# A decoder kernel: the first products of five half tiles cut into 32 columns instead of 64, and another place for one weight tile

## The chip, the cores and the metric

The kernel is one program on one core of a Trainium2 chip. The core has a matrix engine (TensorE, PE in the profile, with PEld for its loading of weights), VectorE (DVE), ScalarE (ACT), GpSimd (POOL) and SyncE (SP), which mainly issues DMAs. The metric is the device time of one execution in microseconds; of several runs the median is given.

## The reference

Two decoder layers work on x of shape (8, 256, 256) in float32. The first has self attention, attention over a context and a choice of experts; the second has causal attention, attention over the context with a learned null key and value, and the feed-forward part that the change touches. That part takes the 2,048 tokens after a layer norm:

```python
scores_aE = x_aD @ router_DE
vals_aK, idx_aK = jax.lax.top_k(scores_aE, K)          # K = 1, E = 8 experts
gates_Ea = jax.nn.sigmoid(masked_aE).T
routed_in_EaD = gates_Ea[:, :, None] * x_aD[None, :, :]
mid_EaF = silu(einsum('ead,edf->eaf', routed_in_EaD, w1_eDF)) * einsum('ead,edf->eaf', routed_in_EaD, w3_eDF)
routed_out_EaD = einsum('eaf,efd->ead', mid_EaF, w2_eFD)
shared_aD = silu(x_aD @ ws1_DF) * (x_aD @ ws3_DF) @ ws2_FD
out_aD = shared_aD + routed_out_EaD.sum(axis=0)
```

D is 256 and F is 704. Every token goes through one expert of eight and through the shared expert, and x is added to the result.

## The kernel before, in words

**The last stage.** Tokens are sorted by expert into tiles of 128 rows. A tile either belongs to one expert as a whole (tiles 0 to 11) or is a half tile, with 64 rows of one expert and 64 of another (tiles 12 to 16). `slots` (L1858) goes through them in the order 0, 1, 12, 2, 3, 13, 4, 5, 14, 6, 7, 15, 8, 9, 16, 10, 11. For every tile `into` (L1829) makes the hidden layer and `outof` (L1842) the output rows, and the next tile's `into` stands ahead of this tile's `outof`. PE and SP run exactly in the order in which the code is written there; the other engines' order is a planner's. Every second tile two tiles of rows are turned by `turned` (xrp in the profile).

Within `into`, `hidden` (L1061) goes through six chunks of 128 hidden units, the last one half wide. A chunk needs two outputs h of 128 x 128 (for w1 and w3; the last has both in one, so there are 11 in all). `first` (L1833) makes an output as a sum over two chunks c of the input's 256 features. In a half tile this is done for each of its two sets of weights, with 64 tokens each. Each such product goes through `product` (L274), which cuts the 128 output columns of the weights into two matmuls of 64 columns on two halves of the output's partitions. The profile calls these "h<-xrT,w" at L276; 128*64 128x64 is a half tile's form, with 64 tokens, and 128*64 128x128 a full tile's. ScalarE then applies silu (sl, L1071), and VectorE multiplies (midr, L1072). `outof` multiplies by the second weights in products of 64 columns, 256 wide (out, L1846).

The weights come from HBM, packed by expert: `first_weights` (L1802) loads w1 and w3 of a set (w13, 1,408 KB) and `second_weights` (L1812) w2 (768 KB), on SP's queue. A half tile takes two sets. There are four buffers of each kind; a load is issued when PE has finished with the buffer that it reuses.

**`product4`** (L280) does what `product` does with four matmuls of 32 columns on four quarters of the output's partitions. It serves the attention (qk, v, ao, fm, vps in the profile at L282), the choice of experts in the first layer (lg, cs, rps, back) and other places. den (L1446) also has 32 columns.

**The shared expert's weights.** When the last of eight batches begins its attention over the context, the projection weights are no longer needed, and L1582 closes the pools that held them. On the right side of the memory they lay, from the top down, as ctxs (4,096 bytes a partition), wp (wkv_x 32,768 and wq_x 8,192, wkv_x below), kvs (kT and vx, 8,192 each, vx above kT), and wsum. L1583 opens a new pool, mids, in their place, with its top where that of ctxs was. Its first tile lies lowest. `load_shared` (L1054) makes its tiles in this order: ws13 (w1 and w3 of the shared expert, 11,776 bytes), two mid (12,288 each) and ws2 (the second weights, 6,144). The routing tables follow (4,448). `ended` (L1033) has POOL clear the part of the last chunk that the weights do not fill. `w_in` (L1025) loads ws13 on SP, `w_out` (L1038) loads ws2 there, later (L1603), and POOL copies 64 columns within ws13 (L1030). Names in the profile drop numbers: ws13 and ws2 both appear as ws, mid0 and mid1 as mid.

The shared expert's first products are hx (L1079) in that stretch, with silu and the products by seven (L1120) behind them; its outputs by ws2 are added at L1674. After the last tile PE makes the last quarter of the shared expert (L1079 and L1663).

Of the kernel before, what the change touches and what calls it, by code (L numbers as in the profile page):

```python
# [29 lines left out]
F32 = mybir.dt.float32  # L30
# [9 lines left out]
P = 128  # L40
B, S, D = 8, 256, 256
# [9 lines left out]
NFC = len(FCH)  # L51
# [106 lines left out]
def plain(  # L158
# [105 lines left out]
    def layernorm_T(b, work, mm, bufs=2):  # L264

        xn = work.tile([P, 2, D], F32, tag="xn", name="xn", bufs=bufs)
        mv, rs = norm_stats([x[:, 2 * b + t, :] for t in range(2)], 1e-5, small, "ln")
        for t in range(2):
            last = normed(xn[:, t, :], x[:, 2 * b + t, :], mv, rs, t)
        return last, transposed(xn, work, mm, "xnT", bufs=bufs)  # L270
# [3 lines left out]
    def product(out, lhsT, rhs, start, stop):  # L274
        return [
            nc.tensor.matmul(out[h], lhsT[:, h], rhs, start=start, stop=stop, skip_group_check=True)  # L276
            for h in (slice(0, 64), slice(64, P))
        ]
# [570 lines left out]
    def context(b):  # L849
        t = ctxs.tile([P, CTX // P, S], F32, tag="ctxT", name="ctxT")  # L850
        nc.sync.dma_start(t, a["ctx_T"][b].rearrange("(c p) t -> p c t", p=P))
        return t

    def key_room():
        return kvs.tile([P, nc8, S], F32, tag="kT", name="kTx")

    def value_room():
        return kvs.tile([P, 2, XH, XD], F32, tag="vx", name="vx")
# [166 lines left out]
    def w_in(pool, src1, src3, name):  # L1025

        t = pool.tile([P, 2, 2 * FF + tail], F32, name=name, tag=name)
        nc.sync.dma_start(t[:, :, :FF], src1.rearrange("(c p) f -> p c f", p=P))
        nc.sync.dma_start(t[:, :, FF + tail :], src3.rearrange("(c p) f -> p c f", p=P))
        nc.gpsimd.tensor_copy(t[:, :, FF : FF + tail], t[:, :, 2 * FF :])  # L1030
        return t

    def ended(t):  # L1033

        nc.gpsimd.memset(t[tail:, full, :], 0.0)
        return t

    def w_out(t, src):  # L1038
        nc.sync.dma_start(t[:, :full, :], src[: full * P].rearrange("(c p) d -> p c d", p=P))
        nc.sync.dma_start(t[:tail, full, :], src[full * P :])  # L1040
        return t
# [5 lines left out]
    shared = {}  # L1047
# [5 lines left out]

    def load_shared(pool):  # L1054

        shared["ws13"] = w_in(pool, a["L1_ffn_ws1_DF"], a["L1_ffn_ws3_DF"], "ws13")

        shared["mid_s"] = [ended(pool.tile([P, NFC, 2 * S], F32, name=f"mid{i}")) for i in range(2)]
        shared["ws2"] = ended(pool.tile([P, NFC, D], F32, name="ws2"))

    def hidden(mid, first, n, pair, silu):  # L1061

# [126 lines left out]
    def routed_norm(b, work):  # L1189

        xn = work.tile([P, 2, D], F32, tag="y", name="xne", bufs=1)
        mv, rs = norm_stats([x[:, 2 * b + t, :] for t in range(2)], 1e-5, small, "ln")
        for kept, v in zip(norms[b], (mv, rs)):
            nc.gpsimd.tensor_copy(kept, v)
        for t in range(2):
            normed(xn[:, t, :], x[:, 2 * b + t, :], mv, rs, t)
        return xn

    def routed_rows(b, xn, work):
        transposed(xn, work, mm, "", shared["xnT"][:, :, bass.ts(b, S)])  # L1200
# [87 lines left out]
    def null_cross_attention(phase):  # L1288
# [15 lines left out]
        def query_room():  # L1304
            return work.tile([P, nc8, S], F32, tag="qT", name="qTx", bufs=1)
# [20 lines left out]
        def w_terms(blocks, m):  # L1326

            ((b11, b12), (b21, b22)), (t1, t2, t3, t4) = blocks
            return [t[:, :, m, :] for t in (b11, b21, b22, t4, t1, t2, t3)]

        def sums_of_rows(rows, n, name, apart):


            def block(i, j):
                return rows[:, n * j : n * (j + 1), bass.ts(i, P)]

            sw = wsum.tile([P, 4 if apart else 3, n, P], F32, tag=name, name=name)
            s1, s2, s4 = (sw[:, i] for i in range(3))
            s3 = sw[:, 3] if apart else block(1, 0)
            nc.vector.tensor_tensor(s1, block(1, 0), block(1, 1), ALU.add)  # L1340
            nc.vector.tensor_tensor(s2, s1, block(0, 0), ALU.subtract)
            nc.vector.tensor_tensor(s4, block(0, 1), s2, ALU.subtract)
            nc.vector.tensor_tensor(s3, block(0, 0), block(1, 0), ALU.subtract)
            return block(0, 0), block(0, 1), s4, block(1, 1), s1, s2, s3
# [168 lines left out]
        def in_range():  # L1513

            for k in range(3):
                v = dens[:, k].rearrange("p t h -> p (t h)")
                low = work.tile([P, S], F32, tag="low", name="lowk", bufs=1)
                nc.vector.tensor_scalar(low, v, 1.0e-25, None, ALU.is_ge)
                nc.vector.scalar_tensor_tensor(
                    low, v, 1.0e25, low, ALU.is_le, ALU.mult, accum_out=fit[:, B + k : B + k + 1]  # L1520
                )
# [46 lines left out]
        for b in range(B):  # L1568
            more = b + 1 < B
            if more:  # L1570
                ctxT = context(b + 1)
            oT, den, rest = weighted(kT, v, qT)
            if more:
                _, xnT = layernorm_T(b + 1, work, mm, 1)
                if b:
                    xe = routed_norm(b - 1, work)
                of_ctx = sums_of_rows(ctxT, CTX // P // 2, "sw", False)
            else:
                xe = routed_norm(b - 1, work)
                rest()  # L1580

                wproj.close()  # L1582
                late = ctx.enter_context(tc.tile_pool(name="mids", bufs=1, side="right"))  # L1583
                load_shared(late)
                sums = phase.enter_context(tc.tile_pool(name="sums", bufs=1, side="right"))
                order.enter_context(tc.manual_schedule(engines={mybir.EngineType.PE}))
            if more:
                order.enter_context(tc.manual_schedule(engines={mybir.EngineType.PE}))
            if b:
                routed_rows(b - 1, xe, work)  # L1590
            if more:
                of_x = sums_of_rows(xnT, 1, "swq", True)
                kT, v, qT = key_room(), value_room(), query_room()
                k7 = seven("k7", of_ctx, w_terms(kv_blocks, 0), kT, False)
                v7 = seven("v7", of_ctx, w_terms(kv_blocks, 1), v, True)
                q7 = seven("q7", of_x, w_terms(q_blocks, 0), qT, False)
                next(k7)
                rest()
            rs, old = reciprocals(b, den, en), en
            if b == 1:  # L1600
                in_range()
            if not more:
                w_out(shared["ws2"], a["L1_ffn_ws2_FD"])  # L1603
                routing_tables(late)
            if more:

                for made in (k7, k7, v7, k7, k7, k7, v7, v7, q7, v7, q7, v7, v7, q7):
                    next(made)
            else:
                first = hidden_shared(0, pair, lambda n: spare()[:, 0, :n])  # L1610
                for i in range(4):
                    next(first)
                    if i == 0:
                        routed_scores(b - 1)
                shared["of_w"] = sums_of_shared(*(sums.tile([P, full * P], F32, name=f"tws{i}") for i in range(4)))
            divide(oT, rs, (nc.gpsimd, nc.gpsimd if more else nc.vector))
            outward(b, oT, old)
            if more:
                next(q7), next(q7)
                if b:  # L1620
                    routed_scores(b - 1)
                next(q7)
                en = null_key(xnT)
            else:
                for _ in first:
                    pass
            order.close()
# [11 lines left out]
    with ExitStack() as phase:  # L1639
        null_cross_attention(phase)  # L1640
# [3 lines left out]
    def token_experts(phase):  # L1644
# [5 lines left out]
        ws2, mid_s = shared["ws2"], shared["mid_s"]  # L1650
# [178 lines left out]
        def into(sets, xrT):  # L1829
            mid_r.append(mid_r.pop(0))  # L1830
            mid, n = mid_r[-1], P // len(sets)

            def first(h, lo):  # L1833
                for i, (w13, _) in enumerate(sets):
                    for c in range(2):
                        product(h[:, bass.ts(i, n)], w13[:, c, lo : lo + P], xrT[:, c, bass.ts(i, n)], c == 0, c == 1)

            for _ in hidden(mid, first, P, pair, silu):
                pass
            return mid  # L1840
# [64 lines left out]
        with tc.issue_after(last.ins), tc.manual_schedule(engines={mybir.EngineType.DVE}):  # L1905
            for i in range(4):
# [3 lines left out]
                if i:  # L1910
                    lo = group[0]
# [946 lines left out]
```

## Time and profile before

| What | us |
|---|---|
| median of 3 runs | 1198.14 |
| lowest and highest of them | 1196.61, 1200.52 |
| profiled execution, its own time | 1198.71 |
| its span, first to last instruction | 1197.0 |
| PE busy in the span | 1135.5 (95%) |
| DVE, ACT, POOL busy | 566.2, 447.5, 417.6 |
| expert tiles on PE, first to last product | 1021.3 to 1158.4 |
| loads of ws13 issued | 915.5 |

Times in the trace are counted from the span's start. A row of the chain of waits gives the start, the length and what ran; "issue" is time for which the profile shows no cause. A row of the groups by form gives line, engine, operation, the tiles written and read, the shape, and how often; then busy time, mean ns of one, idle time before and what ended it. For a matmul 128*64 128x64 means 128 rows and 64 columns of weights and 64 moving columns per partition. Each float32 matmul of the code stands as two in the records. Busy times are unions, and matmuls on different columns overlap, so busy time is less than the sum of the parts. A row of the windows gives the stretch, its length, the busy time and count of each engine (PE, PEld, DVE, ACT, POOL), the granted clock of PE (1.00 is full), the share of the 16 DMA engines and GB/s. In the list of queues stand packets, MB and the share of 16 engines.

### The profile page before, as it was taken

How to read it: one execution, taken by the hardware profiler on the slowest of the kernel's cores; microseconds unless marked ns; L12 is line 12 of the kernel's file. 1: busy time of each engine (PE TensorE's matmuls, PEld its weight loads, DVE VectorE, ACT ScalarE, POOL GpSimd, SP SyncE). 2: the span in 40 equal slices, each digit the busy share in tenths (PEclk: the TensorE clock that was granted, in tenths of full speed). 3: DMA queues.
4: the chain of work that ended last, by engine and by line, in shares of the span. 5: the costliest groups of instructions: out<-in, count | busy, mean ns of one | idle time of the engine just before them, and what ended most of it. 6: DMA issues, size and time to landing. Idle time of an engine off the chain costs nothing.

```text
span 1197.0 us, 31939 instructions
## 1 busy us (share of the span) xinstructions
PE 1135.5 (95%) x13788; PEld 706.5 (59%) x13788; DVE 566.2 (47%) x1564; ACT 447.5 (37%) x696; POOL 417.6 (35%) x482
## 2 busy tenths in 40 slices
PE   6898899998899999999999999999998999999996
PEld 2334444454445454666676767666664576888864
DVE  5465878778685643824241424242324473222213
ACT  3666665665443541314141414141413230222220
POOL 3245365455655730314141414141415114100013
PEclk9999999999999999999999999999998999999999
DMA  7046232130200600020202010101103007799924
GB/s 226 1 133 204 91 119 92 54 122 2 84 2 17 233 3 19 2 54 2 54 2 54 6 50 10 46 19 37 24 15 105 5 30 305 277 414 394 392 73 129
DMA packets 51446, 116.78 MB, mean 98 GB/s; under 512 B 8272, under 2 KB 36416, under 8 KB 46944
## 3 DMA queue, kind: packets, MB, share of 16 engines
q1 hardware_dynamic: 45120, 98.90, 24.0%
q0 software_dynamic: 3456, 12.73, 2.9%
q10 hardware_dynamic: 2720, 3.02, 0.7%
q8 instruction: 110, 1.80, 0.6%
q14 instruction: 40, 0.33, 0.1%
HBM read 104.00 MB, written 27.93 MB: 110 GB/s over the span
## 4 chain that ended last, share of the span: by engine, by line
PE 76%; POOL 7%; issue 6%; DVE 6%; ACT 4%; DMA 1%; SPq 0%; POOLq 0%; ACTq 0%; DVEq 0%
PE h L276 7%; PE k L276 6%; PE v L276 6%; PE wo L276 5%; PE ox L1470 5%; PE stx L1431 5%; PE st L334 4%; PE out L1846 4%; PE o L371 3%; PE out L1663 3%; PE h L1079 3%; PE qk L282 3%; PE q L276 3%; ACT pT L345 2%; PE den L1446 2%
## 5 line engine op out<-in xcount | busy, mean ns | idle before, releaser
L345 ACT ACTIVATE pT<-st 128x1024 f32<-128x1024 f32 (+1 forms) x128 | 110.7, 919 | 64.3 <-PE st L334 64.3
L371 PE MATMUL o<-pT,padv 128*32 128x256 f32 (+1 forms) x1536 | 99.7, 370 | 4.3 <-POOL pT L350 4.2
L371 PEld LDWEIGHTS o<-pT,padv 128*32 128x32 f32 x1536 | 40.6, 109 | 86.2 <-issue 37.5
L1437 POOL TENSOR_TENSOR both<-pTx 128x512 f32<-128x512 f32 x64 | 81.2, 1296 | 29.0 <-ACT pTx L1435 23.8
L276 PE MATMUL h<-xrT,w 128*64 128x128 f32 (+1 forms) x1936 | 87.0, 250 | 0.4 <-issue 0.4
L276 PEld LDWEIGHTS h<-xrT,w 128*64 128x64 f32 x1936 | 84.4, 137 | 3.3 <-issue 1.1
L345 ACT ACTIVATE pT<-st,kbias 128x1024 f32<-128x1024 f32 x64 | 67.9, 1112 | 44.0 <-PE st L334 44.0
L258 POOL TENSOR_TENSOR lnrs<-lnve,mhalf 128x2 f32<-128x2 f32 x48 | 34.7, 723 | 127.8 <-DVE lnve L256 124.1
L1072 DVE TENSOR_TENSOR midr<-sl,h 128x128 f32<-128x128 f32 x102 | 29.4, 288 | 102.5 <-PE h L276 69.9
L1435 ACT ACTIVATE pTx<-stx 128x1024 f32<-128x1024 f32 x64 | 62.1, 1022 | 40.8 <-PE stx L1431 27.7
L1071 ACT ACTIVATE sl<-h 128x128 f32<-128x128 f32 (+1 forms) x114 | 35.4, 311 | 94.7 <-PE h L276 55.7
L334 PE MATMUL st<-qm,kT 32*128 32x512 f32 (+1 forms) x512 | 66.8, 591 | 4.0 <-ACT pT L345 2.0
L1431 PE MATMUL stx<-qTx,kTx 64*128 64x256 f32 x512 | 64.4, 391 | 2.5 <-ACT pTx L1435 2.5
L282 PE MATMUL qk<-l_wqkv,xnT 128*32 128x512 f32 x512 | 63.3, 607 | 0.7 <-ACT xnT L294 0.7
L1470 PE MATMUL ox<-pTx,vx 128*64 128x256 f32 x512 | 62.3, 385 | 0.0
L258 POOL TENSOR_TENSOR lxrs<-lxve,mhalf 128x2 f32<-128x2 f32 x8 | 5.6, 706 | 159.9 <-DVE sc L1210 124.2
L1525 POOL TENSOR_TENSOR oT<-oT,rs 128x512 f32<-128x512 f32 x30 | 37.3, 1273 | 65.0 <-DMA rs<-rd 65.0
L1431 PEld LDWEIGHTS stx<-qTx,kTx 64*128 64x128 f32 x512 | 46.1, 186 | 20.3 <-ACT pTx L1435 7.2
L276 PE MATMUL wo<-wout_x,oT 128*64 128x256 f32 x512 | 58.0, 379 | 0.0
L350 POOL TENSOR_SCALAR_AFFINE_SELECT pT<-pT 128x512 f32<-128x512 f32 x64 | 42.0, 670 | 41.8 <-ACT pT L345 38.7
L1846 PE MATMUL out<-w,midr 128*64 128x256 f32 x408 | 47.1, 379 | 2.7 <-issue 2.7
L1470 PEld LDWEIGHTS ox<-pTx,vx 128*64 128x64 f32 x512 | 33.9, 136 | 26.4 <-issue 12.5
(361 smaller groups left out, 2164.1 us busy)
## 6 DMA issues: line engine op xcount, KB each, us to landing
w<-packs SPq DMA_DIRECT2D x22, 1408.0 KB
w<-packs SPq DMA_DIRECT2D x22, 768.0 KB
rs<-rd SPq DMA_DIRECT2D x16, 512.0 KB
packs<-L_ffn_w_eDF SPq DMA_DIRECT2D x8, 704.0 KB
packs<-L_ffn_w_eDF SPq DMA_DIRECT2D x8, 640.0 KB
packs<-L_ffn_w_eFD SPq DMA_DIRECT2D x8, 640.0 KB
ctxT<-ctx_T SPq DMA_DIRECT2D x8, 512.0 KB
wkv_x<-L_xattn_Wkv POOLq DMA_DIRECT2D x1, 4096.0 KB
```

What stands on the lines that cost most here:

```text
L258: nc.gpsimd.tensor_tensor(rs[:, :n], ve[:, :n], mhalf[:, :n], ALU.pow)
L276: nc.tensor.matmul(out[h], lhsT[:, h], rhs, start=start, stop=stop, skip_group_check=True)
L282: nc.tensor.matmul(out[h : h + HP], lhsT[:, h : h + HP], rhs, start=start, stop=stop, skip_group_check=True)
L334: nc.tensor.matmul(st[:, r, :, :n], self.kT[rows, c, bass.ts(kt, P)], self.qm[rows, :, c, q0:], start=True, stop=True,)
L345: nc.scalar.activation(pT[:, :, :, :n], st[:, 2 * k : 2 * k + 2, :, :n], AF.Exp, scale=self.scale, **kb)
L350: nc.gpsimd.affine_select(out=pT[:, :, :, :P], in_=pT[:, :, :, :P], compare_op=ALU.is_ge, fill=0.0, base=0, pattern=[[0, 2], [0, 2], [1, P ...
L371: nc.tensor.matmul(o[HP * j : HP * j + HP, m, q0:], self.v_pad[:, kt, 8 * c + 2 * j + m, :], pTs[j // 2][:, j % 2, m, : S - q0], start=kt ...
L1431: nc.tensor.matmul(st[:, g, kt, :], kT[rows, c, bass.ts(kt, P)], qT[rows, c, :], start=True, stop=True)
L1435: nc.scalar.activation(pT, st, AF.Exp, scale=scale)
L1437: nc.gpsimd.tensor_tensor(both, pT[:, :, 0, :], pT[:, :, 1, :], ALU.add)
L1470: nc.tensor.matmul(o[XD * g : XD * (g + 1), i, :], v[:, kt, 2 * (c2 + i) + g, :], pT[:, g, kt, :], start=kt == 0, stop=kt == 1, skip_group ...
L1846: nc.tensor.matmul(ps[h], mid[:, i, h], sets[k % len(sets)][1][:, i, :], start=i == 0, stop=i == NFC - 1, skip_group_check=True,)
```

## The change

There are two edits. In a half tile, `first` calls `product4` instead of `product`, so each product is cut into four matmuls of 32 columns. A full tile still uses `product`, and so does `outof`. The result is the same sums.

The tile ws2 is made first in its pool, and is therefore its lowest tile; ws13 and the two mid move up by 6,144 bytes. Its clearing by POOL moves out of `load_shared` to where it is loaded, behind the work on the sums of the last batch's attention.

```diff
     def load_shared(pool):
 
+        shared["ws2"] = pool.tile([P, NFC, D], F32, name="ws2")
         shared["ws13"] = w_in(pool, a["L1_ffn_ws1_DF"], a["L1_ffn_ws3_DF"], "ws13")
 
         shared["mid_s"] = [ended(pool.tile([P, NFC, 2 * S], F32, name=f"mid{i}")) for i in range(2)]
-        shared["ws2"] = ended(pool.tile([P, NFC, D], F32, name="ws2"))
...
             if not more:
-                w_out(shared["ws2"], a["L1_ffn_ws2_FD"])
+                w_out(ended(shared["ws2"]), a["L1_ffn_ws2_FD"])
                 routing_tables(late)
...
             def first(h, lo):
+                made = product if len(sets) == 1 else product4
                 for i, (w13, _) in enumerate(sets):
                     for c in range(2):
-                        product(h[:, bass.ts(i, n)], w13[:, c, lo : lo + P], xrT[:, c, bass.ts(i, n)], c == 0, c == 1)
+                        made(h[:, bass.ts(i, n)], w13[:, c, lo : lo + P], xrT[:, c, bass.ts(i, n)], c == 0, c == 1)
```

## The prediction

> **What bounds the kernel now.** I read the page first, then the chain of waits from 1020 us on, then the groups by form, the windows and the DMA view of the same stretch. The page says that TensorE is the bound, and that one DMA queue carries nothing but instructions.
>
> ```profile
> PE 1135.5 (95%) x13788; PEld 706.5 (59%) x13788; DVE 566.2 (47%) x1564; ACT 447.5 (37%) x696; POOL 417.6 (35%) x482
> ...
> q8 instruction: 110, 1.80, 0.6%
> ```
>
> Each product stands there twice, as a weight load and as a matmul: 27,576 records, 27,815 with PE's 239 semaphore and control instructions. Over 110 packets that is 253 each, so q8 is PE's own instruction stream, in packets of 16 KB and about 250 instructions.
>
> The chain runs on PE alone from 1021 to 1177 us. It shows three holes that no engine and no load released, each in or just after the first products of a half tile (h x176):
>
> ```profile
> 1058.32 5.28 PE h L276 x176
> 1063.60 1.30 PE out L1846 x12
> 1064.89 0.56 issue
> 1065.46 1.51 PE out L1846 x12
> ...
> 1082.50 4.19 PE h L276 x143
> 1086.69 0.43 issue
> 1087.12 1.20 PE h L276 x33
> ...
> 1130.43 5.13 PE h L276 x176
> 1135.56 2.10 issue
> 1137.65 2.81 PE out L1846 x24
> ```
>
> In the trace's records the holes stand after 24,513, 25,281 and 27,073 PE instructions. The distances are 768 and 1,792, which is 3 and 7 times 256: PE stops where a packet of instructions ends. In each case the next q8 packet began late (1063.03, 1084.79, 1135.35 us), took 1.0 to 1.1 us, and PE went on 2.43, 2.33 and 2.30 us after the packet's start. The DMA view narrowed to 1135.2 to 1136.5 us holds exactly that one; the windows show why it is late:
>
> ```profile
> q8 instruction: 1, 0.02, 5.2%
> ```
> ```profile
> 1031.00:1058.00 27.00, 27.00 (x473) 22.89 (x468) 5.76 (x20) 7.36 (x25) 1.07 (x2) 1.00 1.01 414
> ```
>
> The DMA engines are full (share 1.01, 414 GB/s) from 1031 to 1136 us with the experts' weights. Lining up all 110 packets with the count of instructions, a packet is asked for one block of 256 plus some 47 instructions before PE needs it. From asking to start it waits 0.3 to 1.1 us in stages with idle DMA (0.7 typical), 3.3 to 5.7 us here (3.9 typical). With the 2.3 us after the start, code is ready **3.0 us (quiet) or 6.2 us (loaded)** after it is asked for. A full tile spends 224 instructions and 4.9 + 2.6 us, so 303 of them last 10 us and hide 6.2; a half tile's 352 instructions last 5.2 us, 303 of them 4.5 us, and hide it only just. That is why all three holes (3.1 us) are at half tiles.
>
> **The narrower products.** By form, today's are these, beside the shortest products of 32 columns in the trace:
>
> ```profile
> L276 PE MATMUL h<-xrT,w 128*64 128x64 f32 x880 | 26.9, 222 | 0.4 <-issue 0.4
> ```
> ```profile
> L282 PE MATMUL lg<-gate,xnbT 128*32 128x8 f32 x256 | 3.7, 178 | 0.0
> ```
>
> Per half tile there are 11 outputs x 2 sets x 2 chunks x 2 column halves, each recorded twice: 176. The change makes 352, hence 704 instructions for 352; in five half tiles 880 pairs and seven packets are added.
>
> *Array.* Products on different column groups run beside each other: 176 of 64 columns in 5.24 us (mean of the five) are 88 rounds of two, 59.5 ns each; 352 of 32 are 88 rounds of four. Work per round is equal, so nothing is won unless loading 64 columns is what a round waits for. The router's products (64 columns, 8 wide) also take 59 ns a round, so it partly is; the floor is the long products' pace, 216 ns for 256 wide, or 54 ns for 64. Best case: 88 x 5.5 ns = 0.5 us a half tile, **-2.5 us** in all.
>
> *Issue.* The lg batches start four products in 28 to 39 ns while queued instructions last; towards the end of a batch, when new ones have to come in, the last five starts are 17 ns apart (105.747, .764, .781, .798, .814, .832). 352 x 16.7 ns = 5.88 us against 5.24: +0.64 a half tile, **+3.2 us**. The slow end would be today's 14.9 ns per instruction, if that were already the supply's limit: +5.2 a half tile, +26. I take 3.2, since the router's batches of 16, which fit in the queue, show the same 59 ns: 64 columns set today's pace, not the supply.
>
> The Trainium skill (TensorE: Matmul & The Clock Gate, Wait — 56ns, not 53.3ns?) gives about 25 ns as the least distance between starts however small the product. The lg rows go below it, at 7 to 17 ns. By the rule a half tile would take 8.8 us, an estimate from that page, and five would cost +18.
>
> *Switches.* den (32 columns, 8 products, two rounds) takes 0.57 us on the chain where two rounds of 216 ns are 0.43; ox after it 1.88 where eight are 1.73. So about 0.15 us each time the column width changes. out stays at 64, so there are five new switches back and three into (two half tiles follow a transpose of 128 anyway): 8 x 0.15 = 1.2, partly under the slower issue: **+1.0**, between 0 and 1.2.
>
> *Code.* 256 instructions at 8.35 ns last 2.1 us, and 303 last 2.5. 704 are 2.75 blocks, so two block ends fall wholly inside each half tile's products. At the first, loaded: 6.2 - 2.5 = 3.7 us of standing. At the second the next packet is asked for only on entering the block, 2.1 us ahead; meanwhile no buffer comes free, so no new weight load is triggered and the queue drains: 3.0 - 2.1 = 0.9. A stage stretched by 20 us holds DMA at 105 / 125 = 0.84 rather than 1.0, so I take 0.8 of the first: 3.0 + 0.9 = 3.9 a half tile, 19.5, less the 3.1 that are paid at these places today: **+16.4**. Ends: both quiet, (0.5 + 0.9) x 5 - 3.1 = +4; both loaded, (3.7 + 4.1) x 5 - 3.1 = +36.
>
> The Trainium skill (Runtime: NRT & Kernel Launch, Instruction fetch mechanics) says that the sequencer fetches the next 256 instructions while it runs the current ones and that crossing costs next to nothing, being mostly hidden. The three holes contradict it under full DMA. By the rule the code term would be 0 and the sum about +4.
>
> What hides behind PE stays there: silu and the multiply take 0.28 and 0.29 us of a chunk's 0.95, and weights land 8 to 13 us before their use, so neither becomes the bound. After the last tile the chain goes on over PE (quarter 3), so what the stage loses the end loses.
>
> **The weights' place.** One memset of 0.31 us on POOL moves from before the routing tables to beside them; POOL idles 0.30 us before en and 2.27 us after it. The four DMAs stay in their order behind rd on SP. Only the addresses could matter: the shared weights' load starts late, PE stands 3.42 us for it, and the next eight products run at half clock (0.50 from 920 to 924 us).
>
> ```profile
> 915.49 4.35 DMA ws<-L_ffn_ws_DF
> 919.84 0.14 issue
> 919.98 6.62 PE hx L1079 x8
> ```
> ```profile
> 915.52 0.98 POOL L1035 MEMSET mid<- 64x512 f32 x2 [1.81 <-issue]
> ```
>
> By the sizes in the code the new pool (46,944 bytes a partition) reaches 1,888 bytes into vx, read by ox until 915.42; ws13 is lowest and lies there, and with ws2 below it would lie over wkv_x alone, last read at 883.6 us. But the first mid already lies over wkv_x alone, and its memset too waits to 915.52 with POOL free since 913.72. So the whole pool waits for vx, and ws13 will again: **0**. If I am wrong, the 3.42 go and the eight products take 3.5 instead of 6.62: -6.5 us.
>
> **Sum**, on the profiled execution (1198.71 us: span 1197.0 and 1.7 around it): 3.2 + 1.0 + 16.4 + 0 = +20.6, some 1219; the median shown is 0.57 below that execution, so I say **1218**.
>
> **Rivals.**
> (a) *Quiet code.* PE's own standing empties the DMA queue, every fetch takes 3.0 us: 3.2 + 1.0 + 4 = +8, 1206. For it: loads come only when PE frees a buffer. Against: at every one of the 15 fetches from 1031 to 1136 us the wait was 3.3 or more.
> (b) *Nothing to measure.* More code is asked ahead than the records suggest, the holes stay as they are, and issue keeps up with the array: -2.5 to +3, 1198. Against: the three holes at exact multiples of 256.
> (c) *Faster.* The pool's wait is by tile: ws13's load is out of the chain before PE needs it, -6.5, from the point where it is issued before 912 us (4.35 us for the first half, needed at 916.5). It outweighs the products only where code costs nothing: -6.5 - 2.5 gives 1189, and -6.5 + 3.2 + 1.0 gives 1196. Against: mid's memset.
>
> **How the numbers follow.** Forecast (1210 to 1230) 0.70; (a) 0.14; (b) 0.08; (c) 0.05; 0.03 is left for code always loaded, up to 1238. A measurement here tells 0.3% (3.6 us) from no change. Slower: 0.70 + 0.14 + 0.03 = 0.87; same: (b), less a hundredth for its ends, 0.07; faster: (c) and that hundredth, 0.06. The range leaves out (b), (c) and the far end: 1203 to 1230.
>
> **What would show it.** L282 h, 128*32 128x64, x1760 in place of x880; its chain pieces 5.9 us or more; q8 117 packets; "issue" holes of 1 to 4 us, two in each half tile and 256 instructions apart; DMA share near 0.85 between 1031 and 1136. ws again from 915.5 with 3.4 us of standing. It is wrong if half tiles stay at 5.3 us without holes, or if hx starts near 916.6.

## The result and the profile after

The changed kernel takes **1227.88 us** (median of 4 runs, 1225.32 to 1231.51) where the kernel before took 1197.62 on the same chip: ratio 1.0255, 95% interval 1.0238 to 1.0272, 30 us slower. The forecast was 1218 in a range of 1203 to 1230. The profiled execution of the changed kernel took 1227.64 us, with a span of 1225.8.

The page of the changed kernel, engines and instruction queue:

```profile
PE 1145.3 (93%) x14668; PEld 710.2 (58%) x14668; DVE 564.5 (46%) x1564; ACT 447.2 (36%) x696; POOL 418.2 (34%) x482
...
q8 instruction: 117, 1.92, 0.6%
...
L282 PE MATMUL h<-xrT,w 128*32 128x64 f32 x1760 | 32.8, 239 | 22.4 <-issue 22.4
```

880 products and seven packets of code more, as counted. In the last line the figure behind the second bar is the idle time ahead of these products: 22.4 us, and all of it is "issue", so no engine, load or semaphore ended it. The chain of waits of the changed kernel shows where (start, length, what):

```profile
1034.09 1.70 PE h L282 x110
1035.79 0.39 issue
1036.18 1.99 PE h L282 x128
1038.17 4.22 issue
1042.39 3.41 PE h L282 x114
1045.80 3.79 PE out L1847 x24
...
1095.20 2.59 PE h L282 x175
1097.79 3.78 issue
1101.57 2.82 PE h L282 x128
1104.39 0.65 issue
1105.04 1.32 PE h L282 x49
1106.36 2.74 PE out L1847 x24
...
1187.24 19.08 PE h L1079 x44
```

Every half tile has two holes, and between them stand exactly 128 products, 256 instructions: one packet. Each of the ten holes ends 2.30 to 2.61 us after the start of a q8 packet (the one that ends at 1101.57 us after a packet of 1099.27), as the three of the kernel before did. The end of the stage moved from 1158.36 to 1187.24 us. Counted from the start of the first half tile, the stage grew from 123.88 to 153.15 us, +29.3. Adding up the chain's pieces of both kernels by kind, from 1021 us on, splits this: holes 22.4 for 3.1 (**+19.3**), the first products 91.1 for 84.9 (**+6.2**), the outs 48.3 for 44.5 (**+3.8**). Ahead of the stage the two executions are 0.4 us apart, and from its end to the last instruction 0.1.

The last two terms have a cause that the prediction didn't have. Windows of the changed kernel, first half tile (the three figures at the end are granted clock, DMA share and GB/s):

```profile
1034.00:1038.00 4.00, 3.61 (x240) 3.42 (x238) 0.87 (x3) 1.21 (x4) 0.00 (x0) 1.00 1.03 428
1038.00:1042.00 4.00, 0.17 (x14) 0.01 (x2) 0.00 (x0) 0.28 (x1) 0.00 (x0) 0.88 0.79 320
1042.00:1047.00 5.00, 4.61 (x120) 3.94 (x122) 0.86 (x3) 0.55 (x2) 0.00 (x0) 0.50 0.25 49
...
1048.00:1058.00 10.00, 10.00 (x142) 8.20 (x139) 1.73 (x6) 2.72 (x9) 1.07 (x2) 1.00 0.99 400
```

PE stands for 4 us in the second row, and in the third it works at **half clock** (0.50). That is why 114 products take 3.41 us in the chain above where 128 took 1.99, and the out behind them 3.79 instead of 2.59. The clock records show six such stretches in the five half tiles, 3.4 us each (two in a row in the first half tile, one in each of the others).

### The profile page after: what moved, and what is told of

The parts are those of the page before. It is cut to its first block, busy times and chain, and to the rows that moved or that the text cites. A ratio compares the mean times of both kernels' runs of the same rounds, so it can differ in the third digit from the quotient of the medians.

```text
span 1225.8 us, 33696 instructions
## 1 busy us (share of the span) xinstructions
PE 1145.3 (93%) x14668; PEld 710.2 (58%) x14668; DVE 564.5 (46%) x1564; ACT 447.2 (36%) x696; POOL 418.2 (34%) x482
## 4 chain that ended last, share of the span: by engine, by line
PE 76%; issue 7%; DVE 7%; POOL 5%; ACT 4%; DMA 1%; DVEq 0%; POOLq 0%; ACTq 0%; SPq 0%
PE k L276 6%; PE v L276 6%; PE wo L276 5%; PE ox L1470 5%; PE h L276 5%; PE stx L1431 5%; PE st L334 4%; PE out L1847 4%; PE qk L282 4%; PE o L371 4%; PE h L1079 3%; PE out L1663 3%; PE q L276 3%; PE h L282 3%; ACT pT L345 2%
## 5 line engine op out<-in xcount | busy, mean ns | idle before, releaser
L282 PE MATMUL qk<-l_wqkv,xnT 128*32 128x512 f32 x512 | 66.0, 628 | 0.7 <-ACT xnT L294 0.7
L276 PE MATMUL h<-xrT,w 128*64 128x128 f32 x1056 | 60.0, 273 | 0.0
L276 PEld LDWEIGHTS h<-xrT,w 128*64 128x64 f32 x1056 | 57.8, 137 | 2.1 <-ACT yr L1856 0.7
L282 PE MATMUL h<-xrT,w 128*32 128x64 f32 x1760 | 32.8, 239 | 22.4 <-issue 22.4
L1847 PE MATMUL out<-w,midr 128*64 128x256 f32 x408 | 50.5, 400 | 0.0
```

The source lines that it names most:

```text
L282: nc.tensor.matmul(out[h : h + HP], lhsT[:, h : h + HP], rhs, start=start, stop=stop, skip_group_check=True)
L1847: nc.tensor.matmul(ps[h], mid[:, i, h], sets[k % len(sets)][1][:, i, :], start=i == 0, stop=i == NFC - 1, skip_group_check=True,)
```

## Experiments

**Theory C**: code is late under full DMA, and long holes halve the clock behind them. **Rival A**: the products themselves cost it, by issue, column width or waits for other engines, whatever the DMA does. **Rival W**: the weights' place has a part.

### The two edits one by one

`p4_only` is the last hunk of the change alone, `ws2_only` the first two hunks alone.

> Only the first products of the half tiles in 32 columns, the weights' place as before. Theory C (code: PE's instructions come late, block after block, while the DMA engines are full, and PE's clock is halved for a while after each longer hole): all of the change is here, 1225 to 1231 us beside 1197.6 of before, two issue holes in each half tile, 20 to 25 us in all, granted clock 0.87 to 0.95 in the stage. Rival W (the weights' place has a part in it): less than 24 us over before.

> Only the shared expert's second weights lowest in their pool, all products as before. Theory C: within 3 us of before; the shared weights' load issued at 915 to 917 us, PE stands 3 to 4 us for it. Rival W: at least 5 us slower than before, since p4_only is as much below the whole change. If the pool's wait is by tile: 6.5 us faster, hx from 916.6 us.

Measured: `p4_only` 1224.62 us beside 1195.61 of before, ratio 1.0254 (1.0233 to 1.0276), the same ratio as the whole change. (The time lies 0.4 us under the forecast 1225 to 1231, which counted from a kernel before at 1197.6.) `ws2_only` 1194.51, ratio 0.9994 (0.9979 to 1.0009): between 2.5 us faster and 1.1 slower. The page of `p4_only`:

```profile
L282 PE MATMUL h<-xrT,w 128*32 128x64 f32 x1760 | 33.7, 242 | 22.9 <-issue 22.9
```

The chain of `ws2_only` where the shared weights' load is issued, and its timeline of POOL:

```profile
911.21 1.90 PE ox L1470 x16
913.11 0.02 SPq L1028
913.13 0.04 issue
913.17 4.18 DMA ws<-L_ffn_ws_DF
917.35 0.14 issue
917.49 5.37 PE hx L1079 x8
```
```profile
913.21 0.98 POOL L1035 MEMSET mid<- 64x512 f32 x2 [1.80 <-issue]
```

With ws2 lowest the load still leaves only when the last ox has ended (913.11; this execution was 2.3 us ahead of the one of before up to there), and mid's memset waits to the same moment. Rival W falls: the cost is in the products, and the place has at most the 1.1 us that the interval leaves. The eight hx products behind the wait took 5.37 us here and 6.62 before, but 5.37 in `p4_only` and 6.73 in `quiet_before` below too, which both have the old place: the place doesn't set it.

### The same change with the DMA engines idle

Both kernels again, with the experts' weights loaded for the first two tiles alone:

```diff
+        kept = []
         def first_weights(t):
+            if len(kept) == 2:
+                return [(kept[g][0], g) for g in range(1 if t < PAIRED else 2)]
...
+                kept.append((w13, None))
...
         def second_weights(sets):
             for i, (w13, of) in enumerate(sets):
+                if isinstance(of, int):
+                    sets[i] = kept[of]
+                    continue
...
+                kept[len([k for k in kept if k[1] is not None])] = w13, w2
```

> Before, with the experts' weights loaded for the first two tiles alone and kept for all later ones (so the later tiles compute with the wrong experts; loads of some 30 weight sets are left out), which leaves the DMA engines nearly idle in the stage. Theory C: code is ready 3.0 us after it is asked for, 303 instructions of a half tile last 4.5 us, so the three holes of 3.1 us go: 1193 to 1196 us, DMA share under 0.35, no issue hole at a half tile. Rival A (the products themselves set the cost, by their issue, width or waits for other engines; full DMA has no part in it): within 2 us of before.

> The changed kernel with the same loads left out. Theory C: first hole of a half tile 3.0 - 303 x 7.75 ns = 0.65 us, second 3.0 - 1.98 = 1.0 us, so 8.3 us of holes in five half tiles, the products 1 to 2 us slower, and no half clock, as no hole is long: 5 to 13 us over quiet_before, some 1200 to 1208 us, granted clock 1.00 in the stage. Rival A: the difference stays as with full DMA, 27 to 31 us over quiet_before.

Measured: `quiet_before` 1193.19 us, ratio to before 0.9976 (0.9959 to 0.9993); `quiet_after` 1204.02, ratio to before 1.0082 (1.0057 to 1.0106). **The difference is 10.8 us where it is 30 with the loads.** Windows of `quiet_before`, then of `quiet_after`, then the latter's chain in the third half tile:

```profile
1031.00:1136.00 105.00, 105.00 (x1954) 90.42 (x1950) 23.06 (x80) 29.56 (x98) 4.80 (x9) 1.00 0.10 30
```
```profile
1031.00:1136.00 105.00, 96.65 (x2430) 81.85 (x2428) 20.99 (x73) 27.41 (x91) 4.80 (x9) 1.00 0.09 29
```
```profile
1084.24 2.69 PE h L282 x178
1086.93 1.41 issue
1088.34 1.99 PE h L282 x128
1090.34 1.48 issue
1091.81 0.87 PE h L282 x46
```

Without the loads the old products leave no hole (105 us busy of 105). The new ones still have holes, but seven instead of ten, of 1.2 to 1.5 us, 9.9 us in all, and the clock stays at 1.00. By the chains the first products take 1.1 us more than in `quiet_before` and the outs 1.1. Rival A would have kept some 29 us; what it has a right to is these 2.2. The quiet holes are longer than I expected (0.65 and 1.0), and only two of the half tiles have two. For the second, the row tells why: PE enters a block at 1088.34 and goes on with the next at 1091.81, so code asked for at the entry is ready after 3.47 us, not 3.0, and the block lasts 1.99. The same 3.47, less the 2.35 us of 303 instructions, makes 1.1 of a first hole's 1.2 to 1.5; the rest of it is not explained.

### As many instructions, but spread

`p4_full` takes 32 columns in the full tiles and leaves the half tiles as they were:

```diff
+                made = product4 if len(sets) == 1 else product
```

> The other way round: first products of the full tiles in 32 columns, 128 tokens wide (176 for 88 in each of 12 tiles), the half tiles as before. 1056 products are added, more than the 880 of the change, but each block of 256 instructions now lasts 4 to 5 us instead of 2. Theory C: code is late by little at a time, 27 blocks by 0 to 0.7 us, less the 3.1 us of before; no hole over 2 us and no half clock: 2 to 16 us over before. Rival A (each added product costs the same 33 ns, 29 us / 880, by issue, width or switches): 35 us over before.

Measured: 1211.36 us beside 1194.13, ratio 1.0146 (1.0121 to 1.0171), +17 us for 1056 products where the change pays 30 for 880. It is 1 us over what theory C allowed (2 to 16) and half of rival A's 35. By the chains: holes 12.8 us (+9.7), products +2.5, outs +4.4. The chain of `p4_full`, one tile:

```profile
1051.77 4.81 PE h L282 x169
1056.58 2.08 issue
1058.65 0.42 PE h L282 x7
1059.07 4.43 PE out L1847 x24
```

One hole of ten was followed by half clock (the out of 4.43 us, granted clock 0.50 there), although it was 2.08 us long and another of 2.30 was not: "no hole over 2 us and no half clock" was wrong by these. What sets the two apart stands below, under "Holes without late code". Elsewhere the out behind 32-column products took 2.74 us for 2.59, a switch of width worth 0.15 us.

### Fewer instructions

`wide` gives the half tiles products of all 128 columns:

```diff
-                        product(h[:, bass.ts(i, n)], w13[:, c, lo : lo + P], ...
+                        nc.tensor.matmul(h[:, bass.ts(i, n)], w13[:, c, lo : lo + P], ...
```

> Half tiles with products of all 128 columns, 88 for 176, so 176 instructions fewer in each. Theory C: the issue holes at half tiles go (3.1 us). What the array does is open: as before (5.2 us a half tile) if a weight load of 128 columns is hidden, up to 119 ns a product (10.5 us) if it takes twice that of 64 columns: from 3 us faster to 24 us slower, and in neither case a hole. Rival A has no holes to lose by fewer instructions: they stay.

Measured: 1216.71 us, ratio 1.0180 (1.0150 to 1.0210), +22.6 us. The chain of `wide`, first half tile:

```profile
1036.40 9.97 PE h L1839 x88
1046.37 2.74 PE out L1849 x24
```

There is no issue hole from 1020 to 1200 us, at a DMA share of 0.87 between 1031 and 1136: with 176 instructions fewer per half tile, code is never late. But a 128-column product takes 113 ns (9.97 / 88) where a round of two 64-column products takes 59.5. That would fit products that wait for their weights to be loaded, but no run shows the reason. 64 columns remain the better width here.

### Holes without late code

`stalls` is `quiet_before` with PE held up ahead of each half tile by a row of copies:

```diff
+        STALL, ends = [10, 12, 15, 18, 21], []
...
+            if len(sets) == 2:
+                for k in range(STALL.pop(0)):
+                    copy = nc.vector.tensor_copy(xrT, xrT)
+                    if k == 0:
+                        tc.add_manual_dep(copy.ins, ends[-1].ins.name, landed, reason="late on purpose")
...
+            ends.append(last)
```

> Before with the experts' loads left out (as in quiet_before, so later tiles use the wrong experts), and PE held up ahead of the products of the five half tiles by 10, 12, 15, 18 and 21 copies of the tile's input on the vector engine, which makes one hole each of some 1 to 6 us, with no code late and idle DMA. Theory C with the clock as its second part (a long hole itself halves the clock behind it): up to 2 us of hole the products behind it take 5.13 to 5.28 us at clock 1.00; from somewhere between 2 and 3.5 us on, products and out behind the hole take some 2.5 to 3.5 us more in all. Rival (full DMA or late code lower the clock, not the hole): clock 1.00 and 5.13 to 5.28 us behind every hole.

Measured: one run, 1214.47 us. The timeline of PE in `stalls` gives the five holes (in brackets at the end of the line that ends one): 1.48, 1.55, 3.12, 3.52 and 5.08 us. The second and the third, then the chain behind these two, then the windows there:

```profile
1062.98 0.71 PE L276 MATMUL h<-xrT,w 128*64 128x64 f32 x17 [1.55 <-DVE xrT L1851]
...
1089.56 0.65 PE L276 MATMUL h<-xrT,w 128*64 128x64 f32 x15 [3.12 <-DVE xrT L1851]
```
```profile
1062.98 5.35 PE h L276 x176
...
1089.56 6.90 PE h L276 x176
```
```profile
1063.00:1066.00 3.00, 3.00 (x103) 3.00 (x105) 0.57 (x2) 0.83 (x3) 0.00 (x0) 1.00 0.23 78
...
1091.00:1094.00 3.00, 3.00 (x62) 3.00 (x61) 0.40 (x2) 0.55 (x2) 0.00 (x0) 0.50 0.00 0
```

After 1.48 and 1.55 us the products take 5.35; after 3.12, 3.52 and 5.08 they take 6.90, 6.58 and 6.90, at half clock for 3.4 us. The DMA engines are idle and no code is late, so the hole itself does it: a loss of 1.2 to 1.55 us a time (I expected more). No lone hole between 1.55 and 3.12 us was made, so the point where it begins is not settled by this run alone.

The Trainium skill (TensorE: Matmul & The Clock Gate, What's actually happening) says that the array's clock falls to half after an idle window of about 3.4 us. The length of each half-clock stretch agrees. But PE need not stand for that long: 3.12 us sufficed here, 2.08 us did once in `p4_full`, and a hole of 2.02 us did in the changed kernel.

The clock records of all the runs together show what decides. In each execution every change of the clock lies at a whole number of steps of 3.413 us from every other; in the changed kernel's last stage it drops at 1041.08, 1075.21, 1102.52, 1133.24 and 1163.96 us, which are 10, 8, 9 and 9 steps apart. So what counts is how much of one such step PE stands still. From 1020 to 1185 us of the nine profiles here there are 14 steps at full clock in which PE stood for 2.02 us or more, and half clock followed each; it followed none of the others, in which PE stood for 1.99 us at most. Windows of `p4_full` on its own steps (where PE was busy for 1.33 us it stood for the other 2.08):

```profile
1055.79:1059.20 3.41, 1.33 (x38) 0.87 (x28) 0.32 (x2) 0.34 (x2) 0.00 (x0) 1.00 0.83 332
1059.20:1062.61 3.41, 3.41 (x18) 1.96 (x17) 0.29 (x1) 0.20 (x1) 0.00 (x0) 0.50 0.80 239
1120.64:1124.05 3.41, 2.65 (x91) 2.56 (x87) 0.86 (x3) 0.83 (x3) 0.00 (x0) 1.00 0.82 317
1124.05:1127.46 3.41, 1.88 (x32) 1.88 (x33) 0.58 (x2) 0.27 (x1) 0.00 (x0) 1.00 0.38 77
```

The hole of 2.08 us lies within one step, and the clock is at 0.50 in the next. The hole of 2.30 us is split over two, 0.76 and 1.53 us, and nothing follows. The limit of some 2 us is this stage's: in the attention before it, where other products run, the clock also fell behind steps with less standing (1.67 us in the step before 321.76 us in the kernel before).

## Why the prediction was right, and where it was short

**What bounds it** held. PE's instruction stream in packets of 256, late under full DMA, makes the cost: with the loads gone, two thirds of it go, and what is left has 9.9 us of holes of the same kind. One reading of it does not fit its own figures: 4.5 us do not hide 6.2 "only just" but fall 1.7 short, where the three holes were 0.56, 0.43 and 2.10 us.

**Code**, forecast +16.4, measured **+19.3**. That the sum is near is luck in part, because mis-sized parts offset each other. The step "at the first, loaded: 6.2 - 2.5 = 3.7 us" takes it that 303 fast instructions stand ahead of the packet's end. That is so only where the end lies far enough into the half tile: behind 175 and 205 products the first hole was 3.78 and 4.25 us, behind 140 it was 1.99, behind 110 and 112 only 0.39 (the code had been asked for while the tile before was still running). The step "the queue drains: 3.0 - 2.1 = 0.9" holds only behind a long first hole: code was then ready 3.47 and 3.74 us after the block was entered, and as half clock stretched the block to 2.82 and 3.01 us, the second hole was 0.65 and 0.74 (2.02 behind the hole of 1.99). Behind the two short ones the DMA engines were still full, code was ready after 6.2 and 5.9 us, and the second hole was 4.22 and 3.94. So each half tile pays about one loaded wait and one small one, 4.0 to 5.0 us, where 3.9 was forecast. The thinning to 0.8 wasn't there: the DMA share did fall to 0.82 (forecast 0.84), yet the holes that lay wholly in a half tile had their full size.

**Issue**, forecast +3.2 (16.7 ns a product), measured **+1.1**. At full clock 128 products take 1.99 us, 15.5 ns each; the starts at a batch's end were too slow a row. The trace also has one more start among those listed, at 105.767 us; with it the distances there are 14 ns on average, not 17.

The Trainium skill (TensorE: Matmul & The Clock Gate, Wait — 56ns, not 53.3ns?) gives about 25 ns as the least distance between starts. It does not hold for products side by side on four column groups: 128 of them in a row started 15.5 ns apart on average.

**Switches**, forecast +1.0: the outs of `quiet_after` take 1.1 us more in all: 0.6 of it as 2.74 for 2.59 behind four of the half tiles, and 0.5 behind the first, where the out took 3.09.

**The weights' place**, forecast 0: `ws2_only` agrees within its interval, and mid's memset waits there as it did before.

**The missing term** is the clock. The prediction quoted the half clock behind the wait for the shared weights (0.50 from 920 to 924 us) and used it to price the weights' place, but did not put it behind its own holes of 3 to 4 us. Of the +6.2 and +3.8 us in products and outs, 2.2 are issue and switches as in the quiet pair; the other **7.8** are put down to the half clock. The terms are then 1.1 + 1.1 + 19.3 + 7.8 = 29.3 us, the stage's growth; forecast were 20.6. The missing term is 7.8 of these 8.7 us. The median was forecast 9.9 us too low, at 1218 (1219.3 less 0.57 is 1218.7) for 1227.88. That it still lies within the range, 2 us under its end, is luck as far as the clock goes: the room up there was left for late code and not for a slower clock.

**Rivals.** (a), quiet code, was forecast at +8; with DMA idle by force it is +10.8, so the mechanism is real, but it needs idle DMA engines, and here they drained only behind long holes. (b) falls with the holes, (c) with `ws2_only`.

The Trainium skill (Runtime: NRT & Kernel Launch, Instruction fetch mechanics) calls the crossing of a block of 256 instructions mostly hidden. `quiet_before` and `wide`, which have no such hole in the last stage, agree; the changed kernel, with 22.4 us of them, doesn't.

## What to carry to other kernels

Count a kernel's instructions per microsecond, not only their work: where 256 TensorE instructions last less than the time to fetch the next 256 (here 3.5 us with idle DMA, 6.2 with full), cutting products finer costs time even if the array would be no slower. Look for "issue" holes at multiples of 256 instructions, and see whether they vanish when the loads are taken out. And price each hole of 2 us or more with what can come behind it: half clock for 3.4 us, worth 1.2 to 1.7 us a time.

## What the runs showed of the hardware that was not expected

- It looks as if the code of the block after next is not asked for while PE stands at a block's end: behind a hole the next packet started 1.1 us (idle DMA) to 3.8 us (full) after PE had entered the block. The shortest time from entering a block to going on with the next, where PE had to wait, was 3.47 us.
- A hole under 3.4 us can halve the clock, and its length alone doesn't decide: 2.08 us did, 2.30 did not, both in `p4_full`. Within a fixed step of 3.413 us, 2.02 us of standing were enough in this stage and 1.99 were not.
- Products of 128 columns with 64 tokens ran at 113 ns each, 1.9 times the 59.5 ns of two 64-column products beside each other, for the same work.
